# x times the self weight made ahead for four batches, two stores moved to GpSimd's queue, and new ranks, in a two-layer graph kernel

## The chip, the core and the metric

The kernel runs on one core of a Trainium2 chip, in one launch. Its engines are TensorE (PE), VectorE (DVE), ScalarE (ACT), GpSimd (POOL) and SyncE (SP); SP issues nearly all transfers. The metric is the device time of one execution in microseconds (us), lower is better. The time before is the median of three runs. Where the text speaks of the profile, it means one further execution that the hardware profiler recorded.

## The reference

The input x has 16 batches of 1024 nodes with 128 features; adj is a 1024x1024 matrix of zeros and ones with a full diagonal. Two layers follow each other, each with a residual and a layer norm.

```python
def L0(x, adj, Wo, Ws, att_w):                 # attention over the graph
    h = x @ Wo
    u1, u2 = h @ att_w[:128, 0], h @ att_w[128:, 0]
    e = u1[:, idx1] + u2[:, idx2]              # idx1, idx2: fixed pairs of nodes
    e = where(e >= 0, e, 0.1 * e)
    att = softmax(where(adj > 0, e, -9e15), axis=1)
    return einsum('bik,bkl->bil', att, h) + x @ Ws

def step(h):                                   # one of 5 steps of layer 1
    m = einsum('nm,bmd->bnd', adj, h)
    av = concatenate([m, m], -1)               # in_matrix = out_matrix = adj
    u3 = h @ U3.T + b_u3
    z = sigmoid(av @ W3.T + b3 + u3)
    r = sigmoid(av @ W4.T + b4 + u3)
    hv = tanh(av @ W5.T + b5 + (r * h @ U5.T + b_u5))
    return (1 - z) * h + z * hv

x = layernorm(x + L0(x, adj, ...))
x = layernorm(x + five_steps_of_L1(x))
```

The term that the change is about is `x @ Ws` of layer 0, together with the residual `x +`: the kernel computes both as x times `wsi`, where wsi is Ws plus the identity.

## The kernel before, in words

**Layout.** A batch is held with its 128 features on the partitions and its 1024 nodes along the free axis, as two halves of 512 nodes (tiles of 128x512, 256 KB). adj lies on chip for the whole run, together with four tables of sums of its quarters. Products with adj need the nodes on the partitions, so before each product the batch is turned, rounded to a high part (an ACT copy, L578) and its remainder (a DVE subtraction, L582), and each product of a block with a quarter of adj is eight matmuls (two parts by four chunks of 128 nodes, L590).

**Turning.** There are three ways. Four PE transposes against `ident` make the turned half in PSUM (L540). Or DVE transposes in 32x32 blocks (`turn`, L548), SP stores the result to DRAM in four pieces (`away`, L558) and loads it back (`back`, L566). `on_pe(b, what)` says which: by PE for batches 0 and 1 in layer 0, for the last step of batches 13 to 15, and for the pairs and steps that the set TURNED names; by DVE and DMA elsewhere.

**Layer 0, function layer0(b).** Four matmul groups make x times the weights for h and the two attention terms (`hx`). The softmax is factored: exponentials of the nodes (`pb`, `q`), their sums against adj on DVE (`z_`, eight per batch), and reciprocals (`rz`) that scale h into the blocks `blk` (ACT the high part, DVE the remainder). For the left half of nodes PE makes two products `po`, DVE multiplies each by pb and adds them in `yT[0]`; then one matmul `px` = wsi times the left half of x (L883), which DVE adds to yT[0] (L890). For the right half, the matmul wsi times x opens the PSUM bank `po2` (L897), two products are added in the same bank, and ACT copies it to `yT[1]` (L909). A matmul of this 128x512 full-precision shape is two records in the trace. Both halves are turned and normed: statistics on DVE (L496, L498), the power -1/2 on POOL (L502 to L512), and the scale on ACT (L517). The result `y0` is stored to DRAM as `yd` (L953), for the residual of layer 1, and goes on to layer 1.

**Layer 1.** Batches go in pairs. Each of five steps makes the messages m of both batches of a pair (function messages). Most pairs and steps use seven products with the tables of sums, on PSUM banks `a`, `b`, `c`; those named in PLAIN use eight plain products, each batch by itself. Then function gates makes, for each half of each batch, four gate matmuls and more on PE (L1132 the u term, L1142 for r and z, L1158 and L1159 for the candidate), the tanh functions on ACT (L1145, L1167) and the four updates on DVE (L1152, L1170, L1173, L1176). Function leave turns the new state for the next step. After step 5 it loads yd (L1232), adds it (L1243), norms, and stores the output (L1264). The very last pieces use the short norm, scaled by DVE (L523).

**The start.** x of batch 0, adj and the weights are loaded first. Sixty pairs of transposes of `ident` into a PSUM tile that nobody reads (`idle_`, L417), and two fills, keep PE occupied while nothing else is ready.

**What sets the order.** Nothing runs in the order of the Python loops. The functions only hand instructions to a `Plan`: engine, planned length in ns, a rank, what is read and written. `order` simulates all engines, with planned lengths, lags between engines and a count of free tiles per tag, and takes on each engine the ready instruction of the lowest rank. The resulting list is emitted in this order, so each engine's queue, SP's and POOL's too, is fixed and executed in order. The ranks come from `rank_of(b, s)` and `rank0(b)` (ten per pair of batches, 4.2 per step), plus offsets from the dictionary D for each kind of work: m for the copies of messages, pu, pr, pz, pv for gate matmuls, u, r, z, hv, h for what follows them, tr for turning, o, ln, out for the end of a batch, l1 to l8 for the parts of layer 0. LATER is added to the rank of the last batch where it is plain.

```python
def rank_of(b, s):
    return 10 * (b // 2) + 4.2 * s + (LATER if b == B - 1 and plain(b // 2, s) else 0)
```

Of the kernel before, what the change touches and what calls it, by code (L numbers as in the profile page):

```python
# [9 lines left out]
F32 = mybir.dt.float32  # L10
# [3 lines left out]
ALU = mybir.AluOpType  # L14
AX = mybir.AxisListType

P = 128
N = 1024
# [10 lines left out]
LATER = 1  # L29
LATE = 3001  # L30
TURNED = {(0, 0), (0, 1), (7, 1), (7, 2), (7, 3)}
# [105 lines left out]
def kernel(  # L137
# [79 lines left out]
    def exact(pools):  # L217

        def pool(name, bufs, space=None):
# [37 lines left out]
            "yd": (24, [P, HALF], F32, bass.MemoryType.DRAM),  # L257
            "ud": (2, [3, N], F32, bass.MemoryType.DRAM),
# [29 lines left out]
        def pe(*a, **k):  # L288
            plan.add("PE", *a, **k)

        def dve(*a, **k):
            plan.add("DVE", *a, **k)

        def act(*a, **k):
            plan.add("ACT", *a, **k)

        def sp(*a, **k):
            plan.add("SP", *a, **k)


        D = dict(m=0.2, pu=1.4, u=0.4, pr=0.4, pz=1.4, r=1.7, pv=1.2, z=1.1, hv=-0.2, h=1.0, tr=1.2, o=4.4, ln=3.3)
        D.update(out=4.8, l1=-9, l2=-3, l3=-3, l4=-4, l5=-4, l6=-2.5, l7=-1, l8=-2)

# [136 lines left out]

        def own_weights():
            pb_ = ("ps", "g", "b")
            pe(150, -4.6, lambda: column_(pb_, slice(2 * P, 3 * P), 5), reads=[(ws, "b"), (("rz", 0), 1)], writes=[(pb_, 0)])
            dve(160, -4.3, lambda: nc.vector.tensor_copy(bias, T(pb_)[:, 0:5]), reads=[(pb_, 0)], writes=[(("bias",), 0)])
            dve(270, -4.5, self_, reads=[(boot, "ws"), (("ident",), 0), (("zs", 0), NC - 1)], writes=[(("wsi",), 0)])
            dve(1000, -4.2, sums, reads=[(boot, "late"), (("bias",), 0), (("uw",), 0), (("rz", 0), 1)], writes=[(("wm",), 0)])
# [18 lines left out]
        def quarter(i, j):  # L465
            return lambda c: adj[:, 4 * i + c, j * HALF : (j + 1) * HALF]
# [133 lines left out]
        def layer0(b):  # L600
# [274 lines left out]
            def add_():  # L875
# [3 lines left out]
            px = ("ps", "acc", b, "px")  # L879
            pe(  # L880
                F,
                rank,
                lambda: nc.tensor.matmul(T(px), wsi, T(xt)[:, left], start=True, stop=True),  # L883
                reads=[(xt, 0), (("wsi",), 0), (yT[1], "p")],
                writes=[(px, 0)],
            )
# [3 lines left out]
                lambda: nc.vector.tensor_tensor(T(yT[0]), T(px), T(yT[0]), ALU.add),  # L890
# [9 lines left out]
            pe(F, rank, px2_, reads=[(xt, 1), (("wsi",), 0), *begun], writes=[(po2, 0)])  # L900
            for g in range(2):
                pe(
                    8 * R,
                    rank,
                    lambda g=g: product(po2, hl[1][g], quarter(g, 1), False, g == 1),
                    reads=[(k, 4 * g + c, j) for k, j in ((hl[1][g], 0), (hl[1][g], 1), (("A",), 1)) for c in range(4)],
                    writes=[(po2, 0)],
                )
            act(A, rank, lambda: nc.scalar.copy(T(yT[1]), T(po2)), reads=[(po2, 0), (yT[0], "s")], writes=[(yT[1], 0)])  # L909
# [34 lines left out]
            for g in range(2):  # L944
# [8 lines left out]
                sp(450, rank, lambda n=n, g=g: nc.sync.dma_start(T(yd[g]), n()), reads=[(y0[g], 0)], writes=[(yd[g], 0)])  # L953
# [236 lines left out]
        def leave(b, s):  # L1190
# [3 lines left out]
            for g in range(2):  # L1194
# [52 lines left out]
                def at(j, o=o):  # L1247
# [13 lines left out]
                sp(  # L1261
                    450,
                    rank + D["out"],
                    lambda o=o, g=g: nc.sync.dma_start(  # L1264
                        out[b].rearrange("(c p) d -> p c d", p=P)[:, 4 * g : 4 * g + 4, :], T(o)
                    ),
                    reads=[(o, 0)],
                )
# [42 lines left out]

        for c in range(NC):
            adj_tables(c)
# [293 lines left out]
```

## Time and profile before

| | before |
|---|---|
| median of 3 runs | 1465.44 us (1465.43 to 1466.03) |
| profiled execution, its own time | 1465.27 us |
| span of the profiled execution | 1463.4 us |
| mean granted clock of PE | 0.994 |
| PE busy | 1441.3 us, 98%, 5036 matmuls |
| DVE busy | 1157.8 us, 79%, 2761 instructions |
| ACT busy | 892.1 us, 61%, 1782 instructions |
| POOL busy | 159.6 us, 11%, 260 instructions |
| DMA | 165.8 MB, 113 GB/s on average; SP's queue 39% of the 16 engines' span |

The span runs from the first to the last instruction; the time of an execution is 1.9 us longer. Busy shares are averages over stages that differ, and matmuls overlap in PE's pipeline, so a busy PE is not yet a PE at its peak; what it does per microsecond is read from the starts of its instructions. The groups name a line, an engine, an operation, the tiles written and read with buffer numbers left out, the count, the busy time and mean duration of one, and the idle time of that engine just before, with what ended it. The stretches (page and trace) give PEclk, the clock that PE was granted, 1.00 being full.

### The profile page before, as it was taken

How to read it: one execution, taken by the hardware profiler on the slowest of the kernel's cores; microseconds unless marked ns; L12 is line 12 of the kernel's file. 1: busy time of each engine (PE TensorE's matmuls, PEld its weight loads, DVE VectorE, ACT ScalarE, POOL GpSimd, SP SyncE). 2: the span in 40 equal slices, each digit the busy share in tenths (PEclk: the TensorE clock that was granted, in tenths of full speed). 3: DMA queues.
4: the chain of work that ended last, by engine and by line, in shares of the span. 5: the costliest groups of instructions: out<-in, count | busy, mean ns of one | idle time of the engine just before them, and what ended most of it. 6: DMA issues, size and time to landing. Idle time of an engine off the chain costs nothing. (4 is left out here: it accounts for less than half of the span.)

```text
span 1463.4 us, 17722 instructions
## 1 busy us (share of the span) xinstructions
PE 1441.3 (98%) x5036; PEld 903.2 (62%) x5036; DVE 1157.8 (79%) x2761; ACT 892.1 (61%) x1782; POOL 159.6 (11%) x260
## 2 busy tenths in 40 slices
PE   9899999999999999999999999999999999999996
PEld 7666666656666666665666655666556665656663
DVE  7886788878898787877888778886889887766435
ACT  5565665666666665656656666556665766564543
POOL 0202001101011020112101121101300101000101
PEclk9999999999999999999999999999999999999998
DMA  5215434554345442554334543455342454221201
GB/s 194 76 41 158 124 87 144 137 159 121 96 120 165 140 124 78 153 143 131 110 108 124 162 123 89 125 148 166 103 112 82 139 171 115 60 63 37 72 0 31
DMA packets 196863, 165.80 MB, mean 113 GB/s; under 512 B 33599, under 2 KB 149014, under 8 KB 196758
## 3 DMA queue, kind: packets, MB, share of 16 engines
q1 hardware_dynamic: 196194, 163.76, 39.2%
q8 instruction: 41, 0.67, 0.2%
q10 hardware_dynamic: 564, 0.85, 0.2%
q14 instruction: 64, 0.52, 0.1%
HBM read 90.44 MB, written 74.10 MB: 112 GB/s over the span
## 5 line engine op out<-in xcount | busy, mean ns | idle before, releaser
L1158 PE MATMUL ps_g_v<-m,wm 128*128 128x512 f32 x320 | 163.4, 592 | 0.0
L1159 PE MATMUL ps_g_v<-r,u5h 128*128 128x512 f32 x320 | 163.4, 592 | 0.0
L1142 PE MATMUL ps_g_r<-m,wm 128*128 128x512 f32 x320 | 159.8, 594 | 2.8 <-ACT gz L1135 2.5
L1142 PE MATMUL gz<-m,wm 128*128 128x512 f32 x320 | 158.6, 592 | 0.0
L1132 PE MATMUL ps_g_r<-hT,u 128*128 128x512 f32 x320 | 151.6, 592 | 0.0
L1170 DVE TENSOR_TENSOR hv<-hv,hT 128x512 f32<-128x512 f32 (+1 forms) x162 | 110.0, 679 | 49.3 <-ACT hv L1167 48.6
L590 PE MATMUL ps_acc_a<-tab,blk_s 128*128 128x512 f32 x544 | 148.5, 415 | 0.0
L1152 DVE SCALAR_TENSOR_TENSOR r<-r,hT 128x512 f32<-128x512 f32 x160 | 108.8, 683 | 47.8 <-ACT r L1145 47.3
L590 PE MATMUL ps_acc_po<-adj,blk 128*128 128x512 f32 x512 | 142.6, 424 | 0.0
L1145 ACT ACTIVATE r<-ps_g_r,bh 128x512 f32<-128x512 f32 x160 | 109.7, 689 | 46.7 <-PE ps_g_r L1142 45.6
L1145 ACT ACTIVATE z<-gz,bh 128x512 f32<-128x512 f32 x160 | 109.9, 688 | 26.6 <-PE gz L1142 26.1
L590 PEld LDWEIGHTS ps_acc_a<-tab,blk_s 128*128 128x128 f32 x544 | 101.2, 188 | 35.3 <-issue 10.9
L590 PEld LDWEIGHTS ps_acc_po<-adj,blk 128*128 128x128 f32 x512 | 96.0, 188 | 37.5 <-issue 15.1
L1135 ACT COPY gz<-ps_g_r 128x512 f32<-128x512 f32 x160 | 91.2, 571 | 35.8 <-PE ps_g_r L1132 34.0
L1173 DVE SCALAR_TENSOR_TENSOR hv<-z,hv 128x512 f32<-128x512 f32 (+1 forms) x162 | 108.2, 671 | 1.9 <-ACT z L1145 0.9
L1176 DVE SCALAR_TENSOR_TENSOR hT<-hv,hT 128x512 f32<-128x512 f32 (+1 forms) x162 | 108.0, 671 | 1.6 <-PE ps_t L540 0.5
L1159 PEld LDWEIGHTS ps_g_v<-r,u5h 128*128 128x128 f32 x320 | 60.6, 189 | 76.7 <-issue 61.8
L1142 PEld LDWEIGHTS gz<-m,wm 128*128 128x128 f32 x320 | 60.0, 190 | 72.3 <-issue 71.9
L582 DVE TENSOR_TENSOR blk_s<-G,blk_s 128x512 fp32r<-128x512 f32 x136 | 91.2, 678 | 13.7 <-ACT blk_s L578 13.5
L1091 DVE TENSOR_TENSOR m<-m,ps_acc_c 128x512 f32<-128x512 f32 x68 | 46.5, 683 | 67.8 <-PE ps_acc_c L590 36.4
L590 PE MATMUL ps_acc<-adj,blk_h 128*128 128x512 f32 x384 | 98.4, 410 | 1.7 <-DVE blk_h L582 1.5
L1167 ACT ACTIVATE hv<-ps_g_v,nb 128x512 f32<-128x512 f32 x80 | 54.8, 685 | 69.1 <-PE ps_g_v L1159 68.9
(178 smaller groups left out, 2542.5 us busy)
## 6 DMA issues: line engine op xcount, KB each, us to landing
G<-X SPq DMA_DIRECT2D x136, 256.0 KB, 2.9
X<-T SPq DMA_DIRECT2D x536, 64.0 KB, 1.8
yd<-y SPq DMA_DIRECT2D x32, 256.0 KB, 2.8
o_o<-yd SPq DMA_DIRECT2D x30, 256.0 KB, 3.6
out_dram<-o_o SPq DMA_DIRECT2D x30, 256.0 KB, 2.3
D_y<-T_y SPq DMA_DIRECT2D x112, 64.0 KB, 2.1
F_y<-D_y SPq DMA_DIRECT2D x28, 256.0 KB, 2.8
X<-y SPq DMA_DIRECT2D x28, 256.0 KB, 2.4
```

Source lines behind the costliest of these rows:

```text
L582: lambda: nc.vector.tensor_tensor(half(1), src(), half(0), ALU.subtract),
L590: nc.tensor.matmul(T(bank), T(blk)[:, k, c, :], right(c), start=(first and i == 0), stop=(last and i == len(terms) - 1), skip_group_check= ...
L1132: nc.tensor.matmul(T(pr), u3, h(), start=True, stop=True)
L1135: nc.scalar.copy(T(pz), T(pr))
L1142: nc.tensor.matmul(T(p_), wm[:, j, :], T(m), start=False, stop=True, skip_group_check=True)
L1145: nc.scalar.activation(T(t), T(p_), AF.Tanh, bias=bh[:, j : j + 1], scale=0.5 * sg)
L1152: lambda r=r, h=h: nc.vector.scalar_tensor_tensor(T(r), T(r), 1.0, h(), ALU.add, ALU.mult),
L1158: nc.tensor.matmul(T(pv), wm[:, 2, :], T(m), start=True, stop=False)
L1159: nc.tensor.matmul(T(pv), u5h, T(r), start=False, stop=True)
L1170: nc.vector.tensor_tensor(T(hv)[:, w], T(hv)[:, w], h()[:, w], ALU.subtract)
L1173: nc.vector.scalar_tensor_tensor(T(hv)[:, w], T(z)[:, w], 1.0, T(hv)[:, w], ALU.add, ALU.mult)
L1176: nc.vector.scalar_tensor_tensor(h()[:, w], T(hv)[:, w], 0.5, h()[:, w], ALU.mult, ALU.add)
```

## The change

The change has four parts.

1. **Made ahead.** A new function `ahead`, called first, makes wsi early and then, for batches 4 to 7 (AHEAD), loads each half of x into a tile of the tags r and z (gate tiles that are not in use at the start), multiplies it by wsi, lets ACT copy the result into a tile of tag m, and lets SP store it to a DRAM tile PX. In layer0 these batches load PX back into a tile of tag xt instead of making the two matmuls; DVE adds its left half as it added px, and adds its right half to po2 in the place of ACT's copy.
2. **Stores on GpSimd's queue.** The stores of yd (all 32) and of the output (28, all but the last two batches) are issued by POOL instead of SP. The Plan counts 900 ns on POOL for each.
3. **Ranks.** Offsets m, u, pr, z, hv, h, tr, o, ln, l2 and l5 in D are new, and LATER is 3 instead of 1.
4. **Turning.** (7, 1) leaves TURNED: step 1 of batches 14 and 15 is turned by DVE and DMA instead of PE.

```diff
@@ -26,9 +26,10 @@
 LOW, HIGH = -20.0, 100.0
 TINY = 1e-30
 PLAIN = {(0, 0), (0, 1), (0, 2), (7, 2), (7, 3), (7, 4)}
-LATER = 1
+LATER = 3
+AHEAD = range(4, 8)
 LATE = 3001
-TURNED = {(0, 0), (0, 1), (7, 1), (7, 2), (7, 3)}
+TURNED = {(0, 0), (0, 1), (7, 2), (7, 3)}
 IDLE = 60
 
 
@@ -255,6 +256,7 @@
             "D": (6, [P, HALF], F32, bass.MemoryType.DRAM),
             "X": (24, [P, HALF + 16], F32, bass.MemoryType.DRAM),
             "yd": (24, [P, HALF], F32, bass.MemoryType.DRAM),
+            "PX": (len(AHEAD), [P, N], F32, bass.MemoryType.DRAM),
             "ud": (2, [3, N], F32, bass.MemoryType.DRAM),
             "ps": (6, [P, HALF], F32, PS),
             "gz": (2, [P, HALF], F32, PS),
@@ -298,8 +300,8 @@
             plan.add("SP", *a, **k)
 
 
-        D = dict(m=0.2, pu=1.4, u=0.4, pr=0.4, pz=1.4, r=1.7, pv=1.2, z=1.1, hv=-0.2, h=1.0, tr=1.2, o=4.4, ln=3.3)
-        D.update(out=4.8, l1=-9, l2=-3, l3=-3, l4=-4, l5=-4, l6=-2.5, l7=-1, l8=-2)
+        D = dict(m=-0.2, pu=1.4, u=0.8, pr=0.8, pz=1.4, r=1.7, pv=1.2, z=1.3, hv=-0.6, h=1.2, tr=1.6, o=5.0, ln=2.9)
+        D.update(out=4.8, l1=-9, l2=-4, l3=-3, l4=-4, l5=-6, l6=-2.5, l7=-1, l8=-2)
 
         def on_pe(b, what):
 
@@ -438,11 +440,34 @@
             nc.vector.tensor_tensor(bh, bias[:, 0:2], bias[:, 3:4].to_broadcast([P, 2]), ALU.add)
             nc.vector.tensor_scalar(bh, bh, 0.5, None, ALU.mult)
 
+
+        def ahead():
+            dve(270, -8, self_, reads=[(boot, "ws"), (("ident",), 0)], writes=[(("wsi",), 0)])
+            for b in AHEAD:
+                d = ("PX", b)
+                for e in range(2):
+                    bank, px, x = ("ps", "ahead", b, e), ("m", "px", b, e), ("rz"[e], "x", b)
+                    hs = slice(e * HALF, (e + 1) * HALF)
+                    sp(450, -89, lambda x=x, b=b, hs=hs: nc.sync.dma_start(T(x), x_t[b][:, hs]), writes=[(x, "sent")], lag=0)
+                    plan.add("DMA", 4 * 190, -101, lambda: None, reads=[(x, "sent")], writes=[(x, 0)])
+
+                    def px_(bank=bank, x=x):
+                        nc.tensor.matmul(T(bank), wsi, T(x), start=True, stop=True)
+
+                    pe(F, 8000, px_, reads=[(x, 0), (("wsi",), 0)], writes=[(bank, 0)])
+                    act(A, -5.5, lambda bank=bank, px=px: nc.scalar.copy(T(px), T(bank)), reads=[(bank, 0)], writes=[(px, 0)])
+                    sp(
+                        450,
+                        -20,
+                        lambda d=d, px=px, hs=hs: nc.sync.dma_start(T(d)[:, hs], T(px)),
+                        reads=[(px, 0)],
+                        writes=[(d, e)],
+                    )
+
         def own_weights():
             pb_ = ("ps", "g", "b")
             pe(150, -4.6, lambda: column_(pb_, slice(2 * P, 3 * P), 5), reads=[(ws, "b"), (("rz", 0), 1)], writes=[(pb_, 0)])
             dve(160, -4.3, lambda: nc.vector.tensor_copy(bias, T(pb_)[:, 0:5]), reads=[(pb_, 0)], writes=[(("bias",), 0)])
-            dve(270, -4.5, self_, reads=[(boot, "ws"), (("ident",), 0), (("zs", 0), NC - 1)], writes=[(("wsi",), 0)])
             dve(1000, -4.2, sums, reads=[(boot, "late"), (("bias",), 0), (("uw",), 0), (("rz", 0), 1)], writes=[(("wm",), 0)])
 
         def adj_tables(c):
@@ -876,18 +901,29 @@
                 nc.vector.tensor_tensor(T(yT[0]), T(yT[0]), T(yT[1]), ALU.add)
 
             dve(V, rank, add_, reads=[(yT[0], "p"), (yT[1], "p")], writes=[(yT[0], "s")])
-            px = ("ps", "acc", b, "px")
-            pe(
-                F,
-                rank,
-                lambda: nc.tensor.matmul(T(px), wsi, T(xt)[:, left], start=True, stop=True),
-                reads=[(xt, 0), (("wsi",), 0), (yT[1], "p")],
-                writes=[(px, 0)],
-            )
+            px = ("xt", b, "px") if b in AHEAD else ("ps", "acc", b, "px")
+            if b in AHEAD:
+                d = ("PX", b)
+                sp(
+                    450,
+                    rank0(b) + D["l3"],
+                    lambda d=d: nc.sync.dma_start(T(px), T(d)),
+                    reads=[(d, 0), (d, 1), (hx, 3)],
+                    writes=[(px, 0)],
+                    lag=2800,
+                )
+            else:
+                pe(
+                    F,
+                    rank,
+                    lambda: nc.tensor.matmul(T(px), wsi, T(xt)[:, left], start=True, stop=True),
+                    reads=[(xt, 0), (("wsi",), 0), (yT[1], "p")],
+                    writes=[(px, 0)],
+                )
             dve(
                 V,
                 rank,
-                lambda: nc.vector.tensor_tensor(T(yT[0]), T(px), T(yT[0]), ALU.add),
+                lambda: nc.vector.tensor_tensor(T(yT[0]), T(px)[:, left], T(yT[0]), ALU.add),
                 reads=[(px, 0), (yT[0], "s")],
                 writes=[(yT[0], 0)],
             )
@@ -897,16 +933,26 @@
                 nc.tensor.matmul(T(po2), wsi, T(xt)[:, right], start=True, stop=False)
 
             begun = [(hl[1][0], c, 1) for c in range(4)]
-            pe(F, rank, px2_, reads=[(xt, 1), (("wsi",), 0), *begun], writes=[(po2, 0)])
+            if b not in AHEAD:
+                pe(F, rank, px2_, reads=[(xt, 1), (("wsi",), 0), *begun], writes=[(po2, 0)])
             for g in range(2):
                 pe(
                     8 * R,
                     rank,
-                    lambda g=g: product(po2, hl[1][g], quarter(g, 1), False, g == 1),
+                    lambda g=g: product(po2, hl[1][g], quarter(g, 1), b in AHEAD and g == 0, g == 1),
                     reads=[(k, 4 * g + c, j) for k, j in ((hl[1][g], 0), (hl[1][g], 1), (("A",), 1)) for c in range(4)],
                     writes=[(po2, 0)],
                 )
-            act(A, rank, lambda: nc.scalar.copy(T(yT[1]), T(po2)), reads=[(po2, 0), (yT[0], "s")], writes=[(yT[1], 0)])
+            if b in AHEAD:
+                dve(
+                    V,
+                    rank,
+                    lambda: nc.vector.tensor_tensor(T(yT[1]), T(po2), T(px)[:, right], ALU.add),
+                    reads=[(po2, 0), (px, 0), (yT[0], "s")],
+                    writes=[(yT[1], 0)],
+                )
+            else:
+                act(A, rank, lambda: nc.scalar.copy(T(yT[1]), T(po2)), reads=[(po2, 0), (yT[0], "s")], writes=[(yT[1], 0)])
 
             for g in range(2):
                 rank = rank0(b) + D["l5"]
@@ -950,7 +996,15 @@
                 def h(g=g):
                     return T(hT)[:, g * HALF : (g + 1) * HALF]
 
-                sp(450, rank, lambda n=n, g=g: nc.sync.dma_start(T(yd[g]), n()), reads=[(y0[g], 0)], writes=[(yd[g], 0)])
+                plan.add(
+                    "POOL",
+                    900,
+                    rank,
+                    lambda n=n, g=g: nc.gpsimd.dma_start(T(yd[g]), n()),
+                    reads=[(y0[g], 0)],
+                    writes=[(yd[g], 0)],
+                    lag=4000,
+                )
                 if plain(b // 2, 0):
                     split(
                         ("blk", b, "h", 0, g),
@@ -1258,14 +1312,14 @@
                     sign(b),
                     b == B - 1 or b == B - 2 and g,
                 )
-                sp(
-                    450,
-                    rank + D["out"],
-                    lambda o=o, g=g: nc.sync.dma_start(
-                        out[b].rearrange("(c p) d -> p c d", p=P)[:, 4 * g : 4 * g + 4, :], T(o)
-                    ),
-                    reads=[(o, 0)],
-                )
+
+                def out_(o=o, g=g, by=nc.gpsimd if b < B - 2 else nc.sync):
+                    by.dma_start(out[b].rearrange("(c p) d -> p c d", p=P)[:, 4 * g : 4 * g + 4, :], T(o))
+
+                if b < B - 2:
+                    plan.add("POOL", 900, rank + D["out"], out_, reads=[(o, 0)], writes=[((o, "sent"), 0)], lag=2600)
+                else:
+                    sp(450, rank + D["out"], out_, reads=[(o, 0)])
 
 
         def look_at(i):
@@ -1309,6 +1363,7 @@
         def sum_flags():
             nc.tensor.matmul(T(("ps", "t", "flag"))[0:1, 0:2], T(("rstd", "ends"))[:, 0, 3:4], ones, start=True, stop=True)
 
+        ahead()
         for c in range(NC):
             adj_tables(c)
         for c in range(NC // 2):
```

## Prediction

> **What bounds the kernel now.** I read the page's busy times first, then the groups of PE with their shapes, then the timeline of PE, and only then the waits.
>
> ```profile
> PE 1441.3 (98%) x5036; PEld 903.2 (62%) x5036; DVE 1157.8 (79%) x2761; ACT 892.1 (61%) x1782; POOL 159.6 (11%) x260
> ```
>
> PE is busy for 98%, but its ends are modelled, so I count starts. In the timeline a 128x512 matmul of layer 1's gates (two records) starts 0.858 us after the one before it, a product of eight records takes 1.87 (0.234 each), four transposes 0.436 (0.109 each). All of PE's records at these prices make 1433.2 us, and the last of them ends at 1451.9. So PE stood still for only about 18.7 us before its last instruction, and 11.5 us follow it. This kernel is faster only by less PE work, by filling those 18.7 us, or by a shorter tail.
>
> Where they are: 11.3 us lie in the first 51 us, 4.2 us in four stalls near 693, 868, 1042 and 1050 us, 2.6 us at 1449. The groups of PE that the change touches:
>
> ```profile
> L540 PE MATMUL ps_t<-ident,hT 128*128 128x128 f32 x104 | 15.7, 273 | 2.5 <-DVE hT L1176 2.5
> ...
> L897 PE MATMUL ps_acc_po<-xt,wsi 128*128 128x512 f32 x28 | 14.3, 592 | 0.0
> L883 PE MATMUL ps_acc_px<-xt,wsi 128*128 128x512 f32 x28 | 14.3, 591 | 0.0
> ```
>
> The hole near the start, in PE's timeline:
>
> ```profile
> 42.36 1.38 PE L540 MATMUL ps_t_b<-ident,y 128*128 128x128 f32 x4 [2.03 <-ACT y L517]
> 43.60 0.28 PE L666 MATMUL ps_t_u<-ident,u 128*24 128x128 f32 x1
> 44.10 0.68 PE L590 MATMUL ps_acc<-adj,blk_h 128*128 128x512 f32 x1 [0.22 <-ACT blk_h L578]
> 46.29 3.35 PE L590 MATMUL ps_acc<-adj,blk_h 128*128 128x512 f32 x7 [1.51 <-DVE blk_h L582]
> ```
>
> PE waits for batch 0's first layer norm. Seven products take 3.35 us here and not 1.64: the busy times by stretches show the granted clock.
>
> ```profile
> core 0: us, PE busy (x) PEld busy (x) DVE busy (x) ACT busy (x) POOL busy (x), PEclk, DMA share, GB/s
> ...
> 40.84:44.26 3.42, 1.62 (x6) 0.81 (x6) 3.28 (x15) 2.41 (x7) 3.01 (x6) 1.00 0.01 4
> 44.26:47.67 3.41, 1.90 (x4) 1.18 (x5) 3.27 (x12) 2.40 (x6) 0.77 (x2) 0.50 0.23 88
> 47.67:51.08 3.41, 3.41 (x11) 2.73 (x10) 3.38 (x11) 3.29 (x12) 0.00 (x0) 0.50 0.39 151
> ```
>
> From 40.16 to 51.08 PE did 3.3 us of work at full-clock prices, so this hole costs 7.6 us. With 0.5 us of waiting at 25.6 the start loses 8.1.
>
> **What the Trainium skill says.** "TensorE: Matmul & The Clock Gate", "What's actually happening": an idle window of about 3.4 us halves the clock, a busy one restores it. The trace agrees: one slack window ends at 44.26, 6.8 us at 0.50 follow. "DMA: Bandwidth & Descriptors", "Anatomy of one DMA — SWDGE (gpsimd) path": about 2.0 us plus bytes over 436e3; for 256 KB an estimate of 2.6 us. No POOL store is in this trace; the SP stores took 2.8 (yd) and 2.3 us (outputs). The same page, "SWDGE vs HWDGE vs iDMA": GpSimd itself writes the descriptors to SBUF, where VectorE can hold it up. "GPSIMD Engine Reference", "Key points", says why: the two share SBUF interfaces. The trace agrees for ordinary instructions:
>
> ```profile
> 1036.68 4.43 POOL L512 TENSOR_SCALAR rstd_o<-rstd_o 128x4 f32<-128x4 f32 x1
> ```
>
> The median of that line is 0.24 us.
>
> **The change, part by part.**
>
> *Transposes.* (7, 1) leaves TURNED, so step 1 of batches 14 and 15 is turned by DVE and DMA instead: 2 batches x 2 halves x 4 = 16 transposes of 0.109, **-1.7 us** on PE. Added are 4 DVE turns of about 0.68 (the V-class row), 16 stores and 4 loads on SP. Their cover is PE's own order: from the last gate product of batch 14's first half to the first product on its new blocks stand 19 groups, some 19 us by the prices above; the way there takes about 11 (tanh 0.7, three DVE operations and the turn 2.7, stores 1.8, load 2.9, split 1.3, and waits). Price 0; without that cover up to 3 us.
>
> *x times self_w.* Eight matmuls of 0.858, 6.9 us, leave batches 4 to 7 and come back in the first 47 us: by themselves they gain nothing, only what they fill. The order of the changed kernel keeps all 120 idle transposes before them. It puts one where PE waited 0.5 us, one in the middle of batch 0's products, and six in a row (5.15 us) ahead of the first ps_t_b. So PE comes to the six 0.9 us later than it came to the hole (two of 0.86 more, less the wait of 0.5 and a small matmul that moved), at 41.1, and is busy to about 46.2. But now batch 1's products, not batch 0's step 0, come after ps_t_b. They need DVE's splits. On DVE the z sums of batch 1, two table pairs and rz stand before them: from 25.7 (one us earlier than before, two table operations are moved behind) I add 0.68 per 128x512, 0.19 per small row, and get 49.4. On ACT four copies of 0.6 stand before the first y scale and two before the second: y done at 46.7 and 49.4, the first rounded block at 50.5, its remainder at 51.5. PE starts there, having done two ps_t_b (0.9): 4.4 us lost. A slack window again; at half clock to the end of the next busy one I lose 1.6, and 0.4 for the second block. Sum 6.4 against 8.1: **-1.7 us**, bounds -4 (DVE's and POOL's rows at their fastest, no half clock) and +2 (the POOL power of 2.0 us takes 3.2 twice, as its second did here, and a loaded x is late). The six 256 KB loads behind 1 MB on SP end near 25.5 by the 299 GB/s of the first 20 us, just in time for the first.
>
> *Combining.* In those batches DVE adds px (0.68) where ACT copied (0.59): four swaps, on engines at 79% and 61%; price 0, cover the products. To SP come eight loads of x and eight stores of 256 KB in the first stretch, later four loads of 512 KB. The stores wait for ACT's copies; behind them on SP stand the loads of x for batches 4 and 5 and then the ud store of batch 2, whose data I place after 60 us, so price 0; DMA moves 113 GB/s here.
>
> *Stores on GpSimd's queue.* 32 yd and 28 output stores leave SP. There they held up what stood behind:
>
> ```profile
> SPq L953 <- ACT y L517: 79.5, 24, 10.9
> ...
> SPq L1264 <- ACT o_o L517: 46.7, 18, 8.2
> ```
>
> Behind these on SP are the turned stores and G loads; PE did not wait for them, so the relief is worth 0 (at best 1 us). On POOL they stand between the layer norms' powers and wait for ACT's scale. Behind them is the next power, behind that ACT's next scale, and behind that, as ACT goes in order, copies that PE needs:
>
> ```profile
> ACT o_o L517 <- POOL rstd_o L512: 9.3, 5, 2.6
> ...
> PEld ps_g_r L1142 <- ACT gz L1135: 9.2, 11, 1.7
> ```
>
> This is how the stalls of 868 and 1042 arise. POOL is free 89% of the time and the order mostly leaves tens of us between a store and the next power, so I take 0; bounds -4.2 (all four stalls go) and, above, the rival's price.
>
> *Ranks.* They change the order everywhere. Steady PE idle is 4.2 of some 1390 us; I keep 4.2.
>
> *The end.* LATER 3 puts batch 14 ahead of 15. Before, the last gate product of 15 ended at 1446.97 and 1.74 us of PE work stood behind it, while DVE still had 14's layer norm:
>
> ```profile
> 1455.64 1.08 DVE L523 TENSOR_SCALAR o_o<-o_o,mv_o,rstd_o 128x128 f32<-128x128 f32 x4
> ...
> 1456.64 2.13 DVE L523 TENSOR_SCALAR y_o<-y_o,mv_o,rstd_o 128x128 f32<-128x128 f32 x8
> ...
> 1457.77 1.40 SPq L1264 DMA_DIRECT2D out_dram<-y_o  x2
> ```
>
> Tail then: 16.4 us. After: DVE's pieces end 3.6 us after that product, transpose, add, statistics to 6.9, power to 8.3, scale to 9.4, store as before 4.6: 14.0. That is -2.4, less 1.3 us of PE work (14's transpose and a gate) that now comes before: **-1.1**, bounds -2.5 and +1.
>
> **Sum**: -1.7 - 1.7 - 1.1 = -4.5 on the profiled execution's 1465.27 (span 1463.4 and 1.9 around it), which is 0.17 under the median of 1465.44: **1460.9 us**.
>
> **Rivals.** (B) *The six are only carried.* They hold ACT and PE away from batch 0's layer norm, and the start ends as late as before or 2 us later; with some new stall in the middle: 1463 to 1467. For it: PE's work as a whole falls by 1.7 us alone. Against: a hole of 7.6 us is there to be filled. (C) *Slower: GpSimd's queue becomes late.* A store whose descriptors DVE holds up for 2 to 4 us delays the power behind it, ACT stands before a scale, PE loses about 0.9 as at 1042. Eight more such stalls turn -4.5 into +2.9; 20 of 60 stores would give 1465.4 - 4.5 + 18 = 1479, ten 1470. For it: the 4.43 us row, 9 such ACT waits already. Against: the spacing. (D) The new order also removes the four steady stalls: 1457. That px is not made ahead at all can be excluded: the order shows it.
>
> **How the numbers follow.** A measurement of this kernel can tell about 0.2%, 2.9 us, from no change: under 1462.5 is faster, over 1468.4 slower. My case 0.53, B 0.22, C 0.17, D 0.08. Faster: most of mine (0.48), D, and a little of B: 0.58. Same: the rest of mine and of B: 0.25. Slower 0.17. The likeliest case alone spans 1458 to 1463.5; 8 in 10 need 1456.3 to 1468.5.
>
> **What would show it.** Right: L540 ps_t x88; no px rows for four batches, eight rows of the new matmul before 48 us; PE busy 41 to 46; a hole of 4 to 5 us until about 51.5 with PEclk 0.50 in the next stretch; the last DVE scale ending within 11 us of the last gate product. Wrong: PE stalls on ACT gz summing over 8 us, ACT waits for rstd well over 9 times, POOL stores with long spans, or PE's hole at the start longer than 7 us.

## The result, and the profile after

The changed kernel took 1458.78 us (median of 6 runs, 1457.73 to 1460.39) against 1465.43 before (6 runs, 1464.92 to 1466.03): the ratio is 0.9955, 95% interval 0.9942 to 0.9967. That is 6.65 us less, where 4.5 was forecast. The profiled execution took 1457.82 us, its span is 1456.0 (before 1463.4): it is one of the faster three of the six, so the table below adds up to 7.4 us and not to 6.65.

The busy times of the page, for the line that was shown first:

```profile
PE 1437.2 (99%) x5020; PEld 899.1 (62%) x5020; DVE 1166.5 (80%) x2769; ACT 896.2 (62%) x1786; POOL 196.7 (14%) x320
```

PE has 16 records less, POOL 60 more (the stores). As in the prediction I count PE's starts at full-clock prices, and call all other time before PE's last instruction its loss:

| us | before | after | forecast |
|---|---|---|---|
| PE's work at full-clock prices | 1433.16 | 1431.42 | -1.7, measured -1.74 |
| loss up to 70 us | 11.75 | 8.87 | -1.7, measured -2.9 |
| loss from 70 to 1430 us | 4.19 | 1.33 | 0, measured -2.9 |
| the rest: idle at the end, and what follows PE's last instruction | 14.3 | 14.4 | -1.1 with its work term, measured +0.1 |
| span | 1463.4 | 1456.0 | |

The groups of PE (instructions by line, with their shapes):

```profile
L565 PE MATMUL ps_t<-ident,hT 128*128 128x128 f32 x88 | 13.6, 275 | 2.9 <-DVE hT L1230 1.6 <-DVE y_o L1297 1.2
L933 PE MATMUL ps_acc_po<-xt,wsi 128*128 128x512 f32 x20 | 10.2, 592 | 0.0
L919 PE MATMUL ps_acc_px<-xt,wsi 128*128 128x512 f32 x20 | 10.2, 592 | 0.0
...
L455 PE MATMUL ps_ahead<-z_x,wsi 128*128 128x512 f32 x8 | 4.2, 605 | 0.0
L455 PE MATMUL ps_ahead<-r_x,wsi 128*128 128x512 f32 x8 | 4.2, 601 | 1.2 <-DMA r_x<-in_x_dram 1.2
```

The 104 transposes are 88; eight records have left each of the two lines of layer 0 and come back as 16 at L455. The start, in PE's timeline:

```profile
43.44 1.02 PE L455 MATMUL ps_ahead<-r_x,wsi 128*128 128x512 f32 x2
44.30 1.02 PE L455 MATMUL ps_ahead<-z_x,wsi 128*128 128x512 f32 x2
...
47.73 1.02 PE L455 MATMUL ps_ahead<-z_x,wsi 128*128 128x512 f32 x2
48.59 0.86 PE L565 MATMUL ps_t_b<-ident,y 128*128 128x128 f32 x4
50.45 1.38 PE L565 MATMUL ps_t_b<-ident,y 128*128 128x128 f32 x4 [1.00 <-ACT y L542]
51.78 2.52 PE L615 MATMUL ps_acc_po<-adj,blk 128*128 128x512 f32 x9
54.64 0.74 PE L615 MATMUL ps_acc_po<-adj,blk 128*128 128x512 f32 x2 [0.33 <-DVE blk L862]
```

and the same stretches as before, with the granted clock (PEclk, third column from the right):

```profile
44.26:47.67 3.41, 3.41 (x9) 1.52 (x8) 3.34 (x16) 2.35 (x5) 3.00 (x6) 1.00 0.40 154
47.67:51.08 3.41, 2.37 (x9) 1.02 (x7) 3.24 (x10) 3.41 (x10) 1.31 (x3) 1.00 0.60 225
```

Batch 1's products start at 51.78, where 51.5 was forecast. But the six products end at 48.6, not 46.2, so the hole is about 2 us long, not 4.4, and in this execution no stretch is at half clock. PE now also waits for the first early load of x at 25.8, 1.4 us by my count of starts (1.2 as the last idle time in the groups above).

Of the waits that were shown for the steady part, ACT's for POOL's power (in total, times, longest):

```profile
ACT o_o L542 <- POOL rstd_o L534: 3.5, 4, 1.3
ACT o_o L542 <- POOL rstd_o L537: 1.5, 2, 1.2
```

Before, the second of them (there L512) was 9.3 us in 5 waits. POOL's operation that then took 4.43 us three times takes 0.55 us near the same place now:

```profile
861.13 0.55 POOL L537 TENSOR_SCALAR rstd_o<-rstd_o 128x4 f32<-128x4 f32 x1
```

PE's wait for ACT gz (2.5 us in three before) is no longer in its list. The stores on GpSimd's queue, as DMA issues and as time on POOL:

```profile
yd<-y POOLq DMA_DIRECT2D x32, 256.0 KB, 3.0
...
out_dram<-o_o POOLq DMA_DIRECT2D x28, 256.0 KB, 2.8
```

```profile
L1317 POOL DMA_DIRECT2D out_dram<-o_o x28 | 23.1, 826 | 66.0 <-ACT o_o L542 57.8 <-ACT hx L662 6.6 <-ACT blk_x L603 1.5
L1003 POOL DMA_DIRECT2D yd<-y x32 | 19.9, 620 | 80.9 <-ACT y L542 76.3 <-ACT blk L856 4.6
```

They land in 3.0 and 2.8 us (2.8 and 2.3 from SP before), so the estimate of 2.6 that the prediction took was 0.2 to 0.4 short, and they hold POOL for 0.62 and 0.83 us. The end:

```profile
1447.65 1.12 DVE L548 TENSOR_SCALAR y_o<-y_o,mv_o,rstd_o 128x128 f32<-128x128 f32 x4
1449.19 1.12 DVE L548 TENSOR_SCALAR y_o<-y_o,mv_o,rstd_o 128x128 f32<-128x128 f32 x4 [0.43 <-POOL rstd_o L528]
```

The last gate product ends at 1440.90. The last scale ends 9.4 us after it, as forecast; the span ends 5.7 us after the scale, where 4.6 was taken over from before.

### The profile page after: what moved, and what is told of

Read it like the earlier page. It is cut to its first block, busy times and chain, and to the rows that moved or that the text cites. A ratio compares the mean times of both kernels' runs of the same rounds, so it can differ in the third digit from the quotient of the medians.

```text
span 1456.0 us, 17810 instructions
## 1 busy us (share of the span) xinstructions
PE 1437.2 (99%) x5020; PEld 899.1 (62%) x5020; DVE 1166.5 (80%) x2769; ACT 896.2 (62%) x1786; POOL 196.7 (14%) x320
## 5 line engine op out<-in xcount | busy, mean ns | idle before, releaser
L615 PE MATMUL ps_acc_a<-tab,blk_s 128*128 128x512 f32 x544 | 144.6, 407 | 0.0
L615 PE MATMUL ps_acc_po<-adj,blk 128*128 128x512 f32 x512 | 136.9, 415 | 0.3 <-DVE blk L862 0.3
L527 POOL TENSOR_SCALAR rstd_y<-mv_y 128x4 f32<-128x4 f32 x32 | 13.2, 413 | 650.3 <-DVE mv_y L523 649.6
L603 ACT CAST blk_s<-G 128x512 fp32r<-128x512 f32 x136 | 82.0, 618 | 27.5 <-DVE G L1077 26.3
```

The source lines that it names most:

```text
L615: nc.tensor.matmul(T(bank), T(blk)[:, k, c, :], right(c), start=(first and i == 0), stop=(last and i == len(terms) - 1), skip_group_check= ...
```

## The experiments

Seven kernels (names that begin with a_) put one part of the change back to what it was, or add something to the changed kernel; five (b_) put one thing, b_two two, into the kernel before. Since every part goes into the plan, most edits change the order of all later instructions; in b_neg and b_pool they don't, because the plan isn't told (b_neg only gives ACT 31 small operations more). One profile is one execution: those of a_ranks and b_ahead are the slowest of theirs, 3.7 and 2.8 us above the medians, those of a_turned and a_stores are the fastest, 2.0 and 2.2 below, so the ratio decides and the profile tells where the time lies. The table gives the ratio to the kernel before, and from one profiled execution each PE's work and loss, counted as above, and the time from the end of the last gate product to the end of the span.

| kernel | ratio, 95% interval | span | PE's work | loss to 70 | 70 to 1430 | after the last gate |
|---|---|---|---|---|---|---|
| before | 1 | 1463.4 | 1433.2 | 11.8 | 4.2 | 16.4 |
| changed | 0.9955, 0.9942 to 0.9967 | 1456.0 | 1431.4 | 8.9 | 1.3 | 15.2 |
| b_neg | 0.9971, 0.9961 to 0.9982 | 1458.0 | 1433.2 | 10.5 | 0.0 | 16.6 |
| b_turned | 0.9991, 0.9984 to 0.9997 | 1461.9 | 1431.4 | 11.4 | 4.3 | 16.8 |
| b_two | 0.9960, 0.9946 to 0.9973 | 1458.0 | 1431.4 | 11.4 | 0.4 | 16.9 |
| b_ahead | 0.9995, 0.9987 to 1.0003 | 1465.6 | 1433.2 | 12.0 | 5.8 | 16.8 |
| b_pool | 1.0021, 1.0014 to 1.0028 | 1465.7 | 1433.2 | 11.3 | 5.9 | 17.4 |
| a_ranks | 1.0010, 1.0004 to 1.0017 | 1467.8 | 1431.4 | 10.9 | 11.1 | 15.2 |
| a_noahead | 1.0005, 0.9997 to 1.0014 | 1466.0 | 1431.4 | 11.3 | 8.9 | 15.1 |
| a_stores | 0.9966, 0.9952 to 0.9979 | 1455.7 | 1431.4 | 8.0 | 2.7 | 14.3 |
| a_turned | 0.9985, 0.9979 to 0.9992 | 1458.5 | 1433.2 | 9.0 | 2.0 | 15.1 |
| a_later | 0.9975, 0.9965 to 0.9986 | 1459.5 | 1431.4 | 10.7 | 1.8 | 17.7 |
| a_load | 0.9950, 0.9936 to 0.9964 | 1455.6 | 1431.4 | 6.8 | 3.0 | 15.1 |
| a_best | 0.9958, 0.9944 to 0.9972 | 1459.1 | 1431.4 | 8.3 | 5.4 | 14.6 |

**Which part holds the gain? The parts put back one at a time.** My first theory was that each term of the sum belongs to one part: the work to TURNED, the start to the products made ahead, the steady stalls to the new offsets.

a_ranks:

```diff
-        D = dict(m=-0.2, pu=1.4, u=0.8, pr=0.8, pz=1.4, r=1.7, pv=1.2, z=1.3, hv=-0.6, h=1.2, tr=1.6, o=5.0, ln=2.9)
-        D.update(out=4.8, l1=-9, l2=-4, l3=-3, l4=-4, l5=-6, l6=-2.5, l7=-1, l8=-2)
+        D = dict(m=0.2, pu=1.4, u=0.4, pr=0.4, pz=1.4, r=1.7, pv=1.2, z=1.1, hv=-0.2, h=1.0, tr=1.2, o=4.4, ln=3.3)
+        D.update(out=4.8, l1=-9, l2=-3, l3=-3, l4=-4, l5=-4, l6=-2.5, l7=-1, l8=-2)
```

> The changed kernel with the offsets D of before (LATER stays 3). Theory by parts: the new offsets own the three stalls near 693, 868 and 1042 us that are gone after the change, and nothing else; with the old offsets POOL's last power operation again falls into an unbroken string of DVE work (4.4 us), ACT waits 2.6, PE 1.2 each time: some 3 us longer than the changed kernel, ratio to before about 0.9975. Rival, relief of SP's queue: the stalls went because the stores left SP; then the old offsets cost nothing here and the ratio stays at 0.9955. Rival, luck of the re-plan: stalls at other places, of 0 to 4 us in sum, unrelated to this part.

Measured: 1.0010, slower than before, and far more than the 3 us expected. The three old stalls did not come back: no operation of POOL takes over 2 us in this kernel. Instead PE loses 11.1 us at other places, for other reasons (the median stands 8 us above that of the changed kernel by the two ratios). PE's waits:

```profile
PE ps_acc_a L615 <- ACT m L1135: 3.9, 2, 2.2
PE ps_ahead L455 <- DMA r_x<-in_x_dram: 2.4, 1, 2.4
...
PE ps_acc L615 <- DVE blk_h L607: 1.4, 1, 1.4
...
PE ps_g_v L1213 <- DVE r L1206: 0.8, 1, 0.8
```

After the wait for blk_h, PE also ran at half clock from 168.7 to 172.2, which is 1.7 of the 11.1. So the theory by parts fell for the steady stretch, and the third theory, that stalls move with every new plan, held in kind, not in size (11 instead of up to 4).

a_noahead (what wsi needs still comes early):

```diff
-AHEAD = range(4, 8)
+AHEAD = range(4, 4)
...
-            "PX": (len(AHEAD), [P, N], F32, bass.MemoryType.DRAM),
+            "PX": (4, [P, N], F32, bass.MemoryType.DRAM),
```

> The changed kernel with AHEAD empty: all batches make x times the self weight where before did. Theory by parts: the 8 matmuls no longer fill the start; PE is idle or at half clock near 44 to 52 us as before, and PE's loss before 70 us goes from 8.9 back to 11.5: 2.5 to 3 us longer than the changed kernel, ratio 0.9975. Rival, carried only: the start's loss is as short without them, because the new offsets of layer 0 (l2, l5) shortened it: the same as the changed kernel.

Measured: 1.0005. The start is as expected: PE's loss before 70 us is 11.3 again, and the stretches show the hole and the half clock of the kernel before:

```profile
40.84:44.26 3.42, 1.12 (x4) 0.62 (x4) 3.32 (x17) 1.63 (x6) 3.09 (x5) 0.84 0.00 0
44.26:47.67 3.41, 2.76 (x7) 1.65 (x7) 3.27 (x11) 3.41 (x11) 2.03 (x5) 0.50 0.22 81
47.67:51.08 3.41, 3.41 (x13) 2.66 (x12) 3.41 (x11) 3.41 (x13) 0.00 (x0) 0.66 0.70 226
```

The new offsets l2 and l5 without the products don't shorten it, so for the changed kernel "carried only" is out. The other 7.6 us are again stalls of the steady stretch, with the new offsets on a list that they were not chosen for.

a_turned:

```diff
-TURNED = {(0, 0), (0, 1), (7, 2), (7, 3)}
+TURNED = {(0, 0), (0, 1), (7, 1), (7, 2), (7, 3)}
```

> The changed kernel with (7, 1) back among the turned steps: 16 transposes more on PE. Theory by parts: 1.7 us longer than the changed kernel by PE's work (1433.2 against 1431.4), ratio 0.9967. Rival, hidden: the DVE and DMA way of turning costs PE a wait that the transposes save, so 0 to 1 us.

Measured: PE's work is 1.74 us more, stalls 0.7 more, the span 2.5 us longer than that of the changed kernel; the ratio of 0.9985 is 3 in a thousand (4.4 us) above it, where 1.7 us were expected. The work term is confirmed; what makes up the rest of the ratio, this fastest of its executions doesn't show.

a_stores (both stores issued by SP again, in the plan too):

```diff
-                plan.add("POOL", 900, rank, lambda n=n, g=g: nc.gpsimd.dma_start(T(yd[g]), n()), ..., lag=4000)
+                sp(450, rank, lambda n=n, g=g: nc.sync.dma_start(T(yd[g]), n()), ...)
-                    plan.add("POOL", 900, rank + D["out"], out_, reads=[(o, 0)], ..., lag=2600)
+                    sp(450, rank + D["out"], ..., reads=[(o, 0)])
```

> The changed kernel with the yd and output stores back on SP. Theory by parts: PE did not wait for them, so within 1 us of the changed kernel (ratio to before 0.995 to 0.9965), stalls still gone. Rival, relief of SP's queue: the three stalls come back, 3 us longer (ratio 0.9975). Rival, POOL's queue costs something: 1 to 2 us faster than the changed kernel.

Measured: 0.9966; the interval overlaps that of the changed kernel; the span is 0.4 us shorter, but in the fastest of five executions. The move brought nothing that can be seen, in a plan that is another from 79 us on. The shorter tail (14.3 against 15.2) comes back below.

**What made the three steady stalls?** Before, at 862 us, DVE ran seven operations on 128x512 without a gap, from 862.02 to 866.30, and POOL's last operation of a power, begun at 861.97, ended at 866.40, when DVE came to the statistics:

```profile
862.02 0.67 DVE L1023 TENSOR_TENSOR G<-G,G 128x512 f32<-128x512 f32 x1
...
865.63 0.67 DVE L1243 TENSOR_TENSOR o_o<-F,o_o 128x512 f32<-128x512 f32 x1
866.34 0.87 DVE L496 BATCH_NORM_STATS2 stats_o<-o_o 128x6 f32<-128x128 f32 x4
...
861.97 4.43 POOL L512 TENSOR_SCALAR rstd_o<-rstd_o 128x4 f32<-128x4 f32 x1
...
866.44 1.65 ACT L517 ACTIVATE o_o<-o_o,rstd_o 128x128 f32<-128x128 f32 x4 [2.57 <-POOL rstd_o L512]
867.99 0.57 ACT L1135 COPY gz<-ps_g_r 128x512 f32<-128x512 f32 x1
868.62 1.91 PE L1142 MATMUL ps_g_r<-m,wm 128*128 128x512 f32 x3 [0.83 <-ACT gz L1135]
```

ACT waits for it with its scale; behind the scale stands the copy that PE needs. The Trainium skill ("GPSIMD Engine Reference", "Key points") says that the two engines share SBUF interfaces, with contention where a DVE instruction has two SBUF inputs. The rows agree: each of the seven reads two SBUF tiles, the statistics one, and POOL is held to the end of the seven, at 687 and 1037 us as here. b_neg takes that operation away from POOL, and leaves every queue in its order:

```diff
-                    nc.gpsimd.tensor_scalar(r[:, 0, :], r[:, 0, :], -1.0, None, ALU.mult)
...
                 r = T(rstd)
+                if sg < 0:
+                    nc.scalar.mul(r[:, 0, :], r[:, 0, :], -1.0)
```

> The kernel before, with the change of sign of the power (POOL L512, last of four operations for half of the batches) done by ACT at the head of the scale instead; the plan is not told, so every queue keeps its order. Theory, DVE holds up POOL's last operation: that operation took 4.43 us three times, each beside an unbroken string of DVE work, and ACT waited 2.6 us for it. Without it on POOL the stalls at 693, 868 and 1042 us are gone and PE's idle time between 70 and 1438 us falls from 4.2 to under 1; 3 us less, ratio 0.998. Rival, the order of ACT alone: ACT's scale stands ahead of the gz copy anyway and the copy is late by the scale's own 1.65 us; then the stalls stay at about their size and 31 small ACT operations more make it 0 to 2 us slower.

Measured: 0.9971, 4.7 us less in the medians; PE's loss between 70 and 1430 us is 0.0. The same place in ACT's timeline (0.21 us for the sign, and no wait):

```profile
861.09 0.21 ACT L516 ACTIVATE rstd_o<-rstd_o 128x4 f32<-128x4 f32 x1
861.33 1.65 ACT L518 ACTIVATE o_o<-o_o,rstd_o 128x128 f32<-128x128 f32 x4
862.88 0.57 ACT L1136 COPY gz<-ps_g_r 128x512 f32<-128x512 f32 x1
```

That settles these stalls: one small operation on POOL, three times beside an unbroken run of DVE, cost 4.2 us. That the run is what held it rests on the three rows, which begin and end with it. It fits that the three appear again in b_turned and b_pool, where the row of 4.43 us is there too (4.30 to 4.43), and in no other kernel.

**Do the parts add, seen from before?** b_turned and b_ahead put one part each into the kernel before:

```diff
-TURNED = {(0, 0), (0, 1), (7, 1), (7, 2), (7, 3)}
+TURNED = {(0, 0), (0, 1), (7, 2), (7, 3)}
```

> The kernel before with (7, 1) out of TURNED and nothing else. Theory by parts: PE's work falls by 16 x 0.109 = 1.74 us and the way over DVE and DRAM has cover in PE's order: 1 to 2 us less, ratio 0.999. Rival, luck of the re-plan: the work falls by 1.74 but the new order of the second half of the run has stalls that the searched one has not, 2 to 8 us: ratio 1.000 to 1.004.

Measured: 0.9991. The work falls by 1.74, the three stalls stay (PE idle for 0.83 us each time, as before), and behind them nothing new arises. Here the parts add.

b_ahead is the function ahead, its loads and its use in layer0, without the other three parts:

```diff
+AHEAD = range(4, 8)
...
+        ahead()
         for c in range(NC):
             adj_tables(c)
```

> The kernel before with x times self_w of batches 4 to 7 made ahead and nothing else (offsets, stores, TURNED, LATER as before). Theory: the start's gain is owned by this part: no stretch at half clock, PE's loss before 70 us about 9 instead of 11.8; but the offsets were set for another list of instructions, so stalls of several us come in the middle: in all 2 to 8 us slower than before, ratio 1.001 to 1.005. Rival, parts add up: 1463, ratio 0.998, with the steady stalls as before.

Measured: 0.9995, no change. From 26.5 to 70 us PE loses 5.0 instead of 8.0; before 26.5 it loses 7.0 instead of 3.8. PE waits 3.2 us for the first early load of x, and from 30.3 to 33.7 runs at half clock. So the hole was filled, but the loss before 70 is not the 9 expected: with the old offsets the products were carried only. The three stalls are replaced by six others (5.8 in sum). Made ahead alone is worth nothing.

b_two joins b_neg and b_turned:

> The kernel before with two small edits: the change of sign on ACT instead of POOL (all queues in the same order), and (7, 1) out of TURNED. Theory: both add, 4.2 of stalls and 1.7 of PE's work, and one more us as in the first of these alone at the start: profiled 1458 to 1459.5, ratio 0.995 to 0.9965, as fast as the changed kernel without any product made ahead. Rival: with the turned step planned anew the stalls come back elsewhere, 0.998.

Measured: 0.9960, a span of 1458.0. In the ratio these two small edits are as good as the whole change, though the start is not touched: 0.4 us of stalls are left, and 11.4 us of loss at the start.

**What do stores on GpSimd's queue cost?** b_pool issues them from POOL and leaves the orders of PE, DVE and ACT as they were:

```diff
-                sp(450, rank, lambda n=n, g=g: nc.sync.dma_start(T(yd[g]), n()), ...)
+                sp(450, rank, lambda n=n, g=g: nc.gpsimd.dma_start(T(yd[g]), n()), ...)
-                    lambda o=o, g=g: nc.sync.dma_start(
+                    lambda o=o, g=g: (nc.gpsimd if b < B - 2 else nc.sync).dma_start(
```

> The kernel before with the 32 yd and 28 output stores issued on GpSimd's queue, the plan not told: the orders of PE, DVE and ACT are those of before. Theory, stores cost and bring nothing: 1 us around before (ratio 0.999 to 1.001), the three stalls as they were. Rival, GpSimd's queue becomes late: a store that waits for ACT's scale holds up the next power, ACT's waits for rstd rise over 20 us in sum and PE's steady stalls from 4.2 to 8 or more: 1469 or more, ratio over 1.0025. Rival, relief of SP: PE's stalls fall to 0 to 2, ratio 0.998.

Measured: 1.0021, 2.7 us more in the medians, 2.3 in the span: between the first two theories. The three stalls are unchanged; there is one new stall and a longer end. The stall, in four engines' timelines:

```profile
1356.53 1.65 ACT L517 ACTIVATE o_o<-o_o,rstd_o 128x128 f32<-128x128 f32 x4 [1.15 <-POOL rstd_o L512]
...
1361.12 0.23 POOL L502 TENSOR_SCALAR rstd_o<-mv_o 128x4 f32<-128x4 f32 x1 [4.63 <-DVE mv_o L498]
...
1363.38 0.83 POOL L1264 DMA_DIRECT2D out_dram<-o_o  x1 [0.31 <-issue]
...
1366.26 0.32 SPq L1232 DMA_DIRECT2D o_o<-yd  x1
...
1369.00 0.69 DVE L1243 TENSOR_TENSOR o_o<-ps_t,o_o 128x512 f32<-128x512 f32 x1 [7.96 <-ACT z L1145]
...
1371.51 1.13 PE L1159 MATMUL ps_g_v<-r,u5h 128*128 128x512 f32 x2 [1.56 <-DVE r L1152]
```

The scale ended at 1358.2, but on POOL the next power stood ahead of the store and waited 4.6 us for its statistics. So the store left 5 us late and landed at 1366.20, the yd load into the freed tile left only then and landed at 1368.88, the add waited for it (its row names ACT's z, which ended within 0.1 us of that and is no input of it), and behind the add on DVE stood r for PE. It is rival C turned round: not the store held up the power, the power held up the store. In the changed kernel, whose plan counts on POOL's queue, PE has no such wait.

The longer end goes with stores on POOL's queue. From the end of the last scale to the end of the span: 4.6, 4.8, 5.0, 5.1, 5.0 and 5.0 us in before, b_neg, b_turned, b_two, b_ahead and a_stores; 5.6 to 5.9 in b_pool, the changed kernel, a_ranks, a_noahead, a_turned, a_load and a_later, and 5.2 in a_best. Most of it lies at the very end: in the traces' semaphore records, 1.37 or 1.38 us pass between SP's last wait for its transfers and the end in the six kernels without such stores, and 2.04 or 2.05 in those with them (1.69 in a_best).

**LATER.** a_later changes only the order of the end:

```diff
-LATER = 3
+LATER = 1
```

> The changed kernel with LATER 1: only the orders of the last 60 us differ. Theory by the sum of the prediction: batch 14's layer norm is again done after the last gate product; PE's idle time at the end and the tail together grow by about 0.4 to 1.1 us, ratio 0.996. Rival: what LATER moves is only where PE waits; under 0.3 us either way.

Measured: 0.9975. The last scale ends 11.8 us after the last gate product, as before, against 9.4; with 1.30 us of PE's work more behind that product, the net is 1.1 us, the upper end of the expectation. The rest of the span's 3.5 us is not due to the edit: the start has the same order as in the changed kernel and lost 10.7 instead of 8.9. PE's wait for the early load was 2.0 us there, not 1.2, and behind it came a stretch at half clock:

```profile
24.15:27.56 3.41, 1.38 (x13) 1.18 (x12) 2.83 (x15) 0.89 (x3) 0.00 (x0) 1.00 1.01 362
27.56:30.97 3.41, 3.41 (x15) 1.89 (x16) 0.63 (x3) 1.17 (x3) 0.00 (x0) 0.50 0.73 244
```

In a_turned, again with the same order, it is the hole at 48 us that halves the clock:

```profile
47.93:51.35 3.42, 2.34 (x10) 1.04 (x8) 2.96 (x7) 3.42 (x11) 1.23 (x2) 1.00 0.65 245
51.35:54.76 3.41, 3.41 (x9) 2.73 (x9) 3.18 (x10) 3.41 (x13) 0.12 (x1) 0.50 0.29 114
```

**The wait for the early load.** a_load:

```diff
-                    plan.add("DMA", 4 * 190, -101, lambda: None, reads=[(x, "sent")], writes=[(x, 0)])
+                    plan.add("DMA", 2200 if (b, e) == (4, 0) else 4 * 190, -101, lambda: None, reads=[(x, "sent")], writes=[(x, 0)])
```

> The changed kernel with the planned landing of the first of the eight early loads set 1.4 us later, so that the plan puts the first two products made ahead some 7 us later and PE no longer waits for that load at 25.8 us (1.4 us). Theory, the end of the hole at 51.8 us is set by the chain of DVE and ACT for batches 0 and 1: PE arrives earlier and waits longer, the loss before 70 us stays within 0.5 us of 8.9. Rival, the wait for the load is lost time of its own: the loss before 70 us falls by 1.4, to 7.5.

Measured: the loss before 70 us is 6.8, so my theory was wrong and the rival right. PE's timeline shows the reason: the whole chain moves with PE.

```profile
31.67 1.13 PE L455 MATMUL ps_ahead<-r_x,wsi 128*128 128x512 f32 x2
...
48.39 1.38 PE L565 MATMUL ps_t_b<-ident,y 128*128 128x128 f32 x4 [1.04 <-ACT y L542]
49.73 2.52 PE L615 MATMUL ps_acc_po<-adj,blk 128*128 128x512 f32 x9
```

The products of batch 0, which stood behind the wait, feed DVE and ACT; they come earlier, and batch 1's products start 2.05 us earlier, with the same wait of 1.0 before ps_t_b. But the steady stretch of this plan loses 3.0 instead of 1.3, and in the ratio (0.9950) it can't be told from the changed kernel. a_best adds the sign on ACT to it:

> The changed kernel with the later planned landing of the first early load and the change of sign on ACT. Theory: the stalls at 314, 504 and 693 us that remain there (1.2 us in sum) follow ACT waits for POOL's power and go or shrink; PE's steady stalls 3.0 to 1.5 to 2, 1456, ratio 0.9935 to 0.995. Rival: ACT's 31 operations more cost as much as they bring, 1457.5, ratio 0.995.

Measured: 0.9958, no better. The stalls at 504 and 693 are gone, that at 314 is not, and there are two larger ones. PE lost 1.1 at 610 us; shortly before, at 593.1, the first operation of another power on POOL took 4.17 us and ACT waited 4.1 for that power, but that the one comes from the other isn't shown. At 164 us DVE waits for a load of adj for its count, and PE behind it, in an order that a_load has too:

```profile
163.53 0.43 DVE L1346 TENSOR_SCALAR junk_look<-look 128x512 f32<-128x512 f32 x1 [4.21 <-DMA look<-in_adj_dram]
...
167.16 1.19 PE L616 MATMUL ps_acc<-adj,blk_h 128*128 128x512 f32 x4 [2.70 <-DVE blk_h L608]
```

In the changed kernel the wait for that load was 2.0 us, and PE lost 0.5 behind it. So part of this stretch varies from one execution to the next.

## Why the prediction was right, point by point

- **Direction and mechanism** were right: less work on PE and a start filled by products made ahead. The forecast of -4.5 is two thirds of the 6.65 measured. That it came so near is in part luck: in the profiled pair the start gained 1.2 us more than forecast and the end 1.2 us less, and the two cancel; the stalls make up what is left.
- **Transposes, -1.7:** -1.74 in the changed kernel, in b_turned and, with the other sign, in a_turned. The price 0 for the added DVE turns and transfers held: b_turned has no new stall over 0.1 us.
- **Start, -1.7:** -2.9. The second block's wait was 0.49 where 0.4 was forecast. The mis-sized term is the half clock: 1.6 us were booked for it, and PEclk stayed at 1.00. That is luck of the execution: a_turned, with the same order, has the half clock just where it was forecast, and a_later has one earlier; either costs about 1.7 us. The hole itself is 2 us, not 4.4, in all of them: the chain on DVE and ACT is shorter than I had summed it. So the date of batch 1's products (51.5 forecast, 51.78 measured) was right by two errors, since PE came late, in part by the wait for the early load, which the prediction did not have, and the chain was shorter; a_stores, with the same order there and no wait for the load, has them at 50.95, and a_load, with the first two products later, at 49.73. How large the gain is, is not exact: with the start's order unchanged, five profiles of the kernel before and its variants lose 10.5 to 11.8, four with the order of the changed kernel 8.0, 8.9, 9.0 and 10.7. The means differ by 2.1. The mean granted clock fits: it is 0.994 in all 13 executions of a_noahead, and 0.995 or 0.996 in the six of the changed kernel, where the three at 0.995 are 1.2 us longer on average. Nor is the gain the products' alone: with the old offsets (a_ranks, b_ahead) the start loses 10.9 and 12.0.
- **Stalls kept at 4.2:** this step failed; 1.33 were left. I had read the row of 4.43 us, but only as a threat to the new stores (rival C), and booked rival D at 0.08. There are also three such stalls and not four, of 1.4 us each by PE's starts: near 1050 PE stands still nowhere. The three equal rows in one profile, a pair of batches (174 us) apart, belonged to the old plan; the new plans of a_ranks, a_noahead and b_ahead don't have them, and b_turned, whose order is the old one up to 1308 us, has. What was not to be had from the trace is what the new plan puts in its place: 1.3 us with this change, 5.8, 8.9 and 11.1 in those three.
- **Stores at 0:** for the steady stretch a_stores shows nothing against it, though in another plan. Their price is at the end, 0.8 us between the changed kernel and a_stores and 1.0 between b_pool and before, and was in no bound of mine.
- **End, -1.1:** about 0. The scale ends 9.41 us after the last gate product (9.4 forecast), and PE's work behind it is 1.30 less. But the term "store as before 4.6" was 5.7, and that eats the gain.
- **Combining at 0:** DVE is 8.7 us busier, and no wait of PE names these additions; shown only in sum.
- **Rivals:** B is out for the changed kernel (a_noahead), but describes b_ahead. C did not occur in the changed kernel; b_pool shows that it is real where the plan doesn't count on the queue. D came true by two thirds.

What stays open: how much of the steady gain belongs to the new offsets. They keep stalls low for this list of instructions and not for others, but other offsets on this list were tried once only. Open too is what share of the start's gain an average execution keeps.

## What to carry to other kernels

Where a planner writes the order, an edit has two effects: what it takes from the bound engine, which can be summed from rows, and a new order, whose stalls can't; so compare variants with the plan untouched (b_neg, b_pool) before giving a part the credit. Look for long rows of a small operation that recur at equal distances: two engines that hold each other up there may cost more than a new algorithm brings. An instruction that is moved to a less busy queue still waits behind what stands in that queue: name its neighbour there. And the same wait near the start may halve the clock in one execution and not in the next, so judge a start by several.

## What the runs showed of the hardware

- A POOL operation on 128x4 that takes 0.24 us (the median) took 4.43 us three times in one execution, each time until an unbroken run of seven DVE operations with two SBUF inputs each ended.
- With stores on GpSimd's queue the end of a program was longer, though the last stores are SP's: in b_pool the span ends 5.63 us after the last scale, in before 4.62; 0.67 of this lies behind SP's last wait.
- The clock: all its changes in one trace lie whole multiples of 3.41 us apart, from a start that differs from one execution to the next. That agrees with the Trainium skill ("TensorE: Matmul & The Clock Gate", "What's actually happening"), which tells of windows of about that length. Laid from these changes, the stretches of 3.41 us at full clock, between 8 and 1430 us of all traces here, part by PE's work in them, at full-clock prices: the largest that was followed by 0.50 had 1.52 us (a_later from 24.15), the smallest that was followed by 1.00 had 1.60 (the changed kernel's hole, from 49.70). A record is counted where it starts, so each figure can be off by up to 0.4. The busy time of the profile doesn't part them: 2.34 in a_turned was followed by 0.50, 1.59 in a_best (from 165.33) by 1.00.
